# Layer 0's output turned by DMA and VectorE on its way to layer 1, with TensorE's steps put in a new order

## The chip, the cores and the metric

The kernel runs on one core of a Trainium2 chip. The metric is the device time of one execution in microseconds. The kernel before takes 2156.92 us, the median of three runs (2154.6 to 2158.59).

## What is computed

A stack of four graph layers over 128 graphs of 64 nodes with 256 features each, in float32. Each layer adds its result to its input and normalises every row:

```
x = layernorm(x + L0(x))     # attention over all node pairs that the adjacency allows, one head
x = layernorm(x + L1(x))     # attention over a list of 512 edges, four heads
x = layernorm(x + L2(x))     # graph convolution, two dense layers with batch normalisation
x = layernorm(x + L3(x))     # two graph convolutions, then four short LSTMs over windows
```

Only layers 0 and 1 matter here. Layer 0 computes, with `Wh = x W`,

```
e = leaky_relu(s1[i] + s2[j]);  e = -inf where adj is 0
x1 = layernorm(x + softmax(e) Wh)
```

Layer 1 starts with two products of `x1`, the queries `x1 W_lin^T` and the values `x1 W_val^T`. Per edge and head it forms leaky-relu scores, takes a softmax over the edges of one source node, sums the weighted values, and multiplies by `W_out^T`.

## The kernel before

**Tiles.** The 8192 rows (graph and node) are cut into NQ = 16 tiles q of 512 rows, held "token-major" as four blocks of 128 rows by 256 features. One tile is 8 graphs (GQ). A big SBUF tile `A` has a slot of 1024 floats per partition for each q; the slot takes layer 0's output of that q (`token_major`, line 208), later layer 2's input. A matmul contracts over partitions, so both layers first need their tile turned: features on the partitions, rows along the free axis (`xT`).

**How it is turned.** There are two ways in the code. `transposed` (line 198) has TensorE make eight 128x128 transposes (line 204) into two PSUM banks, and ScalarE copy them out (line 205). The other is used for layer 0's input from q=1 on: `load_x` (line 126) loads x twice, once plainly into `xin`, and once with eight DMAs (lines 131 to 135) that place each 32x32 square of x, as it is, where the transposed square belongs, in slot q of `A`; then VectorE turns all squares with one `transpose` (line 220), which works within squares of 32x32. Layer 1's tile is turned by TensorE for every q (`l1_t`, line 283).

**Steps.** For layer 0: `l0_a` turns, `l0_b` multiplies by W (16 matmuls, line 230), `l0_c` makes scores and exponentials (one TensorE transpose, line 241; VectorE lines 244 to 248, 254; ScalarE line 251), `l0_d` transposes the exponentials (line 260), `l0_e` multiplies by Wh (line 270), adds x on VectorE and normalises: statistics on VectorE (lines 92 to 95), a power and the scaling on GpSimd (lines 83, 97), into slot q of `A`; last it asks for x of q+2. For layer 1: `l1_t` turns, `l1_qv` makes queries and values in two halves (lines 295 and 298), `l1_graph` one graph's edge scores (two matmuls, line 332, and a ScalarE pass, line 334), `sums` adds them over heads (line 323). Two tiles q form a superblock S of the softmax: `l1_softmax` (line 342 on TensorE, scans on VectorE, lines 344 to 351, an exponential on ScalarE), `l1_sums` (two more scans, lines 357 and 358), `l1_weights` (two sets of transposes, line 366; VectorE lines 372 and 374; four indirect stores into a DRAM table by GpSimd, line 378; two loads back, line 384). Three or four iterations later `v_a`, `v_b`, `v_c` weight the values, multiply by W_out (line 413), add and normalise (line 415 and the layernorm) and store the result (line 418), and prepare layer 2's input (line 433).

**Order.** The loop over q (lines 659 to 676) goes through eight graphs b. After each `l1_graph` it makes the steps of `between[b]`. `step` (line 643) ties every step's TensorE instructions behind the last one of the step before, so TensorE's order is exactly the one written. On the other engines a scheduler in the compiler sets the order, by the order of tracing and by what it reckons to be ready; each engine then works through its list in order. SyncE issues almost all DMAs, also in order.

**Buffers.** PSUM's eight banks: three named "m", which nearly all steps share in turn, two pairs named "z" and one named "e". `tT`, the turned tile, has one buffer that both layers use; `xin` has two.

Of the kernel before, what the change touches and what calls it, by code (L numbers as in the profile page):

```python
# [8 lines left out]
F32 = mybir.dt.float32  # L9
# [8 lines left out]
P = 128  # L18
NB = 128
N = 64  # L20
D = 256
KD = D // P
# [4 lines left out]
NQ = 16  # L27
PQ = 4
QT = 512
# [12 lines left out]
def kernel(ctx: ExitStack, tc: tile.TileContext, i, out):  # L42
    nc = tc.nc
# [4 lines left out]
    dram = ctx.enter_context(tc.tile_pool(name="dram", bufs=1, space=DRAM))  # L48
# [3 lines left out]
    A = main.tile([P, NQ, 2 * QT], F32, name="A")  # L52
# [59 lines left out]
    with ExitStack() as two:  # L112
        wa = two.enter_context(tc.tile_pool(name="wa", bufs=1))
        values, ph = ExitStack(), ExitStack()
        vp = values.enter_context(tc.tile_pool(name="vp", bufs=1, side="right"))
        psm = values.enter_context(tc.tile_pool(name="psm", bufs=1, space=PSUM, side="right"))
        xp = ph.enter_context(tc.tile_pool(name="xp", bufs=2))
        work = ph.enter_context(tc.tile_pool(name="work", bufs=2))
        ps = ph.enter_context(tc.tile_pool(name="ps", bufs=1, space=PSUM))

        def bank(shape, name="m", bufs=3):
            return (psm if name == "m" else ps).tile([P] + shape, F32, name=name, bufs=bufs)

        xin = {}

        def load_x(q):
            xin[q] = xp.tile([P, PQ, D], F32, name="xin")
            nc.sync.dma_start(xin[q], x_view[q])
            if q:

                rows = i["x"][q * QT:(q + 1) * QT, :].rearrange("(j t) (k i f) -> i k t j f", t=32, k=KD, f=32)
                for n in range(4):
                    for k in range(KD):
                        to = A[n * 32:(n + 1) * 32, q, k * QT:(k + 1) * QT]
                        nc.sync.dma_start(to.rearrange("t (j f) -> t j f", f=32), rows[n, k])

        class su:

# [27 lines left out]
        for s in range(2):  # L166
            nc.sync.dma_start(bd[s * N:(s + 1) * N, s * N:(s + 1) * N], i["adj"])
        load_x(1)

        wq = wa.tile([P, KD, D + HEADS], F32, name="wq")  # L170
        wv = wa.tile([P, KD, D], F32, name="wv")
# [22 lines left out]
        def own(q, shape, name):  # L194

            return work.tile(shape, F32, name=name, bufs=1) if q else su.tile(shape, F32, name)

        def transposed(src, q=1):

            t = own(q, [P, KD, QT], "tT")  # L200
            for k in range(KD):
                p_ = bank([PQ, P])
                for c in range(PQ):
                    nc.tensor.transpose(p_[:, c, :], src[:, c, k * P:(k + 1) * P], ident)
                nc.scalar.activation(t[:, k, :], p_.rearrange("p c t -> p (c t)"), AF.Copy)
            return t

        def token_major(q):

            return A[:, q, :].rearrange("p (c d) -> p c d", c=PQ)  # L210


        L0 = {}

        def l0_a(q):
            L0[q] = {"x": xin.pop(q)}
            if q:

                L0[q]["xT"] = work.tile([P, KD, QT], F32, name="tT", bufs=1)
                nc.vector.transpose(L0[q]["xT"].rearrange("p k t -> p (k t)"), A[:, q, :])  # L220
            else:
                L0[q]["xT"] = transposed(L0[q]["x"], q)

        def l0_b(q):
            xT = L0[q]["xT"]
            wh = L0[q]["wh"] = own(q, [P, PQ, D + 2], "wh")
            for c in range(PQ):
                p_ = bank([D + 2])
                for k in range(KD):
                    nc.tensor.matmul(p_, xT[:, k, c * P:(c + 1) * P], w0[:, k, :],  # L230
                                     start=k == 0, stop=k == KD - 1)
                nc.scalar.activation(wh[:, c, :], p_, AF.Copy)

            sb = L0[q]["sb"] = own(q, [P, PQ, P], "sb")
            nc.scalar.activation(sb, wh[:, :, D + 1:].to_broadcast([P, PQ, P]), AF.Copy)

        def l0_c(q):
            wh, sb = L0[q]["wh"], L0[q]["sb"]
            sc = bank([PQ, P])
            for c in range(PQ):  # L240
                nc.tensor.transpose(sc[:, c, :], sb[:, c, :], ident)
            e = L0[q]["e"] = work.tile([P, PQ, P], F32, name="e0")
            for c in range(PQ):
                nc.vector.scalar_tensor_tensor(e[:, c, :], sc[:, c, :], wh[:, c, D:D + 1], mask,
                                               op0=OP.add, op1=OP.add)
            nc.vector.scalar_tensor_tensor(e, e, SLOPE, e, op0=OP.mult, op1=OP.max)
            mx = small.tile([P, PQ], F32, name="mx")
            nc.vector.tensor_reduce(mx, e, AX.X, OP.max, negate=True)
            sm = small.tile([P, PQ], F32, name="sm")
            for c in range(PQ):  # L250
                nc.scalar.activation(e[:, c, :], e[:, c, :], AF.Exp, bias=mx[:, c:c + 1],
                                     accum_out=sm[:, c:c + 1])
            ri = L0[q]["ri"] = small.tile([P, PQ], F32, name="ri")
            nc.vector.reciprocal(ri, sm)
# [9 lines left out]
        def l0_e(q):  # L264
            x, wh, eT, ri = (L0[q][n] for n in ("x", "wh", "eT", "ri"))
            for c2 in range(2):
                p_ = bank([2, D])
                for c in range(2):
                    g = 2 * c2 + c
                    nc.tensor.matmul(p_[:, c, :], eT[:, g, :], wh[:, g, :D], start=True, stop=True)  # L270
                for c in range(2):
                    g = 2 * c2 + c
                    nc.vector.scalar_tensor_tensor(x[:, g, :], p_[:, c, :], ri[:, g:g + 1], x[:, g, :],
                                                   op0=OP.mult, op1=OP.add)
            layernorm(token_major(q), x, PQ, nc.gpsimd)
            L0.pop(q)
            if q + 2 < NQ:
                load_x(q + 2)


        L1 = {}

        def l1_t(q):
            L1[q] = {"xT": transposed(token_major(q)), "qs": [],
                     "v": vp.tile([P, PQ, D], F32, name="v", bufs=5)}

        def l1_qv(q, c2):
            xT, v = L1[q]["xT"], L1[q]["v"]

            sp = spads[q // BPS % 2].rearrange("p (s e x b d h) -> p s e x b d h", e=2, s=2, x=2, b=BPS, d=2)  # L290
            pv = bank([2, D])
            for c in (2 * c2, 2 * c2 + 1):
                pq = bank([D + HEADS])
                for k in range(KD):
                    nc.tensor.matmul(pq, xT[:, k, c * P:(c + 1) * P], wq[:, k, :],  # L295
                                     start=k == 0, stop=k == KD - 1)
                for k in range(KD):
                    nc.tensor.matmul(pv[:, c % 2, :], xT[:, k, c * P:(c + 1) * P], wv[:, k, :],  # L298
                                     start=k == 0, stop=k == KD - 1)
# [235 lines left out]
        setup_order()  # L535
        l0_c(0)
        l0_a(1)
        setup_ends()
        l0_b(1)
# [98 lines left out]
        LAG = BPS + 1  # L638
# [20 lines left out]
        for q in range(NQ):  # L659
            S = q // BPS - 1 if q % BPS == 0 else -1  # L660
            between = [
                [(l0_e, q + 1), (l0_a, q + 2)],
                [(sums, q if q else -1), (l1_softmax, S)],
                [(l1_sums, S), (l0_b, q + 2)],
                [(v_b, q - LAG - 1)],
                [(l1_weights, S), (l1_t, q + 1), (l0_c, q + 2)],
                [(sums, q), (l1_qv, q + 1, 0)],
                [(v_c, q - LAG - 1), (v_a, q - LAG)],
                [(l0_d, q + 2), (l1_qv, q + 1, 1)],
            ]  # L670
# [64 lines left out]
        q = 0  # L735
# [90 lines left out]
    work = ctx.enter_context(tc.tile_pool(name="work3", bufs=2, reuse_waits="tile"))  # L826
# [290 lines left out]
```

## Time and profile before

| | |
|---|---|
| time, median of 3 runs | 2156.92 us |
| TensorE matmuls busy | 2066.8 us (96%) |
| VectorE busy | 881.6 us (41%) |
| ScalarE busy | 931.1 us (43%) |
| GpSimd busy | 418.7 us (19%) |
| packets under 512 bytes | 150192 of 232637 |
| loop over q | 50.98 us (first graph of q=0) to 517 us (last) |
| TensorE, VectorE busy in 223.17 to 255.92 us (q=6) | 30.29 and 23.15 of 32.75 us |
| one turn on VectorE, 128x1024 (line 220) | 1245 ns |
| one transpose on TensorE, 128x128 (line 204) | 273 ns, median |

The profile is one execution. Busy shares are averages over stages with different limits, so a change in one stage is read from that stage alone, here from the timelines of the engines between 50 and 520 us. In a timeline, each row is a group of like instructions: start, time from the first start to the last end, engine, line and operation, tiles, count, and in brackets how long the engine stood idle before it and what ended the wait. Matmuls overlap in the records, so the cost of a group on TensorE is read from its start to the next group's start.

### The profile page before, as it was taken

Reading aid. Unit: us, or ns where it says so; the run is one execution under the profiler, and the core shown is the slowest. Engines: PE = TensorE matmul, PEld = TensorE weight load, DVE = VectorE, ACT = ScalarE, POOL = GpSimd, SP = SyncE. Lnnn points to the kernel's source line nnn. Section 1 sums busy time; section 2 is a strip of 40 time slices with the busy share of each in tenths; the row PEclk is TensorE's granted clock in tenths of the full one; section 3 lists DMA queues with packets and bytes.
Section 4 is the critical chain, followed back from the end, with each engine's and each line's share of the span. In section 5 each row is a group of like instructions: output and inputs, shape, how many; then the busy total and the mean of one; then the engine's idle time right before and its main releaser. Section 6 shows DMA issues by size and latency. Waiting matters only on the chain.

```text
span 2156.5 us, 29415 instructions
## 1 busy us (share of the span) xinstructions
PE 2066.8 (96%) x11343; PEld 1329.6 (62%) x11343; DVE 881.6 (41%) x2069; ACT 931.1 (43%) x1795; POOL 418.7 (19%) x569
## 2 busy tenths in 40 slices
PE   5999999998999979999999999999999999999998
PEld 4666767665544444685576576577477478468466
DVE  7456665654444344233234233323323423423223
ACT  2776666664349064333334234334333333333332
POOL 1133334333200011021111111111111211202012
PEclk8999999999999979999999999999999999999999
DMA  5244531322240022012012112111201202202001
GB/s 154 51 68 80 85 58 48 53 40 43 44 123 20 0 88 79 1 55 81 22 50 69 40 34 64 59 29 55 74 11 59 88 6 60 72 1 59 20 3 56
DMA packets 232637, 113.42 MB, mean 53 GB/s; under 512 B 150192, under 2 KB 215728, under 8 KB 232240
## 3 DMA queue, kind: packets, MB, share of 16 engines
q1 hardware_dynamic: 230640, 109.57, 20.1%
q8 instruction: 89, 1.46, 0.3%
q0 software_dynamic: 1024, 1.05, 0.2%
q10 hardware_dynamic: 832, 0.92, 0.1%
q14 instruction: 52, 0.43, 0.1%
HBM read 67.45 MB, written 44.04 MB: 52 GB/s over the span
## 4 chain that ended last, share of the span: by engine, by line
PE 81%; DVE 7%; ACT 5%; DMA 3%; issue 2%; POOL 1%; SPq 0%; ACTq 0%; DVEq 0%; POOLq 0%
PE l L982 32%; PE l L988 19%; PE pz L719 5%; PE pz L784 4%; PE e L323 3%; PE g L921 2%; PE g L933 2%; PE m L295 2%; PE z L332 2%; PE m L298 2%; PE m L230 2%; PE g L878 1%; PE m L413 1%; DMA way<-st 1%; ACT A L891 1%
## 5 line engine op out<-in xcount | busy, mean ns | idle before, releaser
L982 PE MATMUL l<-H,wih 128*128 128x256 f32 (+2 forms) x2496 | 789.2, 471 | 11.3 <-DVE H L1011 6.1
L982 PEld LDWEIGHTS l<-H,wih 128*128 128x128 f32 x2496 | 469.9, 190 | 304.2 <-issue 188.7
L988 PE MATMUL l<-hid,whh 128*128 128x256 f32 (+2 forms) x1536 | 436.2, 437 | 1.2 <-DVE hid L1011 1.2
L988 PEld LDWEIGHTS l<-hid,whh 128*128 128x128 f32 x1536 | 291.8, 190 | 130.0 <-issue 61.2
L994 ACT ACTIVATE gate_i<-l,bias 128x256 f32<-128x256 f32 (+2 forms) x176 | 100.0, 568 | 515.1 <-PE l L988 440.3
L997 DVE TENSOR_TENSOR gate_i<-gate_i,gate_g 128x256 f32<-128x256 f32 (+2 forms) x96 | 48.4, 504 | 423.6 <-ACT gate_g L994 423.6
L998 POOL TENSOR_TENSOR cell<-gate_f,cell 128x256 f32<-128x256 f32 (+2 forms) x96 | 84.2, 877 | 666.1 <-ACT gate_f L994 666.1
L83 POOL TENSOR_TENSOR ln_rs<-ln_rs,mhalf 128x2 f32<-128x2 f32 (+2 forms) x97 | 78.0, 804 | 662.8 <-DVE ln_rs L95 662.5
L334 ACT ACTIVATE u<-z 128x1024 f32<-128x1024 f32 x128 | 130.3, 1025 | 64.3 <-PE z L332 63.3
L994 ACT ACTIVATE gate_g<-l,bias 128x256 f32<-128x256 f32 (+2 forms) x176 | 100.2, 569 | 100.3 <-PE l L982 52.0
L1002 ACT ACTIVATE gate_g<-cell 128x256 f32<-128x256 f32 (+2 forms) x176 | 90.0, 511 | 90.4 <-DVE cell L999 44.7
L994 ACT ACTIVATE gate_o<-l,bias 128x256 f32<-128x256 f32 (+2 forms) x176 | 99.2, 564 | 62.0 <-PE l L988 54.1
L719 PE MATMUL pz<-A,w 128*128 128x512 f32 x256 | 113.1, 595 | 0.0
L1001 DVE TENSOR_TENSOR cell<-gate_i,gate_g 128x512 f32<-128x512 f32 (+2 forms) x80 | 50.2, 627 | 142.5 <-ACT gate_g L994 142.3
L332 PE MATMUL z<-gath_r,qs 128*128 128x512 f32 x256 | 100.9, 482 | 0.6 <-ACT u L334 0.4
L306 DVE TENSOR_TENSOR qs<-m,qs 64x256 fp32r<-64x256 f32 x128 | 54.1, 422 | 109.0 <-ACT qs L305 106.9
L719 PEld LDWEIGHTS pz<-A,w 128*128 128x128 f32 x256 | 47.9, 190 | 55.4 <-issue 53.4
L295 PE MATMUL m<-wq,tT 128*128 128x260 f32 x256 | 72.5, 407 | 8.1 <-ACT yT L403 5.4
L994 ACT ACTIVATE gate_f<-l,bias 128x256 f32<-128x256 f32 (+2 forms) x96 | 51.0, 531 | 60.0 <-PE l L988 60.0
L1011 DVE TENSOR_TENSOR hid<-gate_o,gate_g 128x256 f32<-128x256 f32 (+2 forms) x96 | 48.4, 504 | 67.5 <-ACT gate_g L1002 39.5
L1011 DVE TENSOR_TENSOR H<-gate_o,gate_g 128x512 f32<-128x512 f32 (+1 forms) x64 | 40.9, 640 | 80.0 <-PE l L982 67.8
L721 DVE BATCH_NORM_STATS2 st<-pz 128x6 f32<-128x512 f32 x64 | 44.4, 697 | 59.5 <-PE pz L719 59.4
(242 smaller groups left out, 2518.4 us busy)
## 6 DMA issues: line engine op xcount, KB each, us to landing
way<-st SPq DMA_DIRECT2D x59, 256.0 KB
st<-way SPq DMA_DIRECT2D x236, 64.0 KB
xin<-in_x SPq DMA_DIRECT2D x16, 512.0 KB
ld<-table SPq DMA_DIRECT2D x16, 512.0 KB
x_dram<-y SPq DMA_DIRECT2D x16, 512.0 KB
x2r<-x_dram SPq DMA_DIRECT2D x32, 256.0 KB
x_dram<-A SPq DMA_DIRECT2D x64, 128.0 KB
x3r<-x_dram SPq DMA_DIRECT2D x64, 128.0 KB
```

The costliest lines, as they stand in the source:

```text
L83: nc.gpsimd.tensor_tensor(dst, dst, mhalf[:, :n], OP.pow)
L295: nc.tensor.matmul(pq, xT[:, k, c * P:(c + 1) * P], wq[:, k, :], start=k == 0, stop=k == KD - 1)
L332: nc.tensor.matmul(z[:, k, :], L1[q]["qs"][c][:, s, k * P:(k + 1) * P], gath_r, start=True, stop=True)
L334: nc.scalar.activation(u, z, AF.Relu)
L719: nc.tensor.matmul(p_, w1[:, k, m * P:(m + 1) * P], A[:, q, k * QT:(k + 1) * QT], start=k == 0, stop=k == KD - 1)
L784: nc.tensor.matmul(p_, w2[:, k, m * P:(m + 1) * P], hidden(q, k), start=k == 0, stop=k == M1 - 1)
L982: nc.tensor.matmul(gates[n], wih[p][:, k, mw * P:(mw + 1) * P], Hw[:, k, :, s, :], start=k == 0, stop=not s and k == KD - 1)
L988: nc.tensor.matmul(gates[n], whh[p][:, k, m * P:(m + 1) * P], hid[:, k], start=False, stop=k == KD - 1)
L994: nc.scalar.activation(act[n], gates[n], AF.Tanh if n == "g" else AF.Sigmoid, bias=bias[:, p - 1, m:m + 1])
L998: nc.gpsimd.tensor_tensor(cell[:, j], act["f"], cell[:, j], OP.mult)
L1002: nc.scalar.activation(act["g"], cell[:, j], AF.Tanh)
L1011: nc.vector.tensor_mul(Hw[:, jj, :, s, :] if over else new[:, jj], o, t)
```

## The change

Layer 1 gets its turned input as layer 0 does, from q=2 on (TURN = 2; q=0 and 1 keep TensorE's transposes, in both layers). `l0_e(q)` writes its normalised tile to a DRAM tile x1 and loads it back with the eight square-placing DMAs, into slot q+1 of `A` (or, for the last two q, a buffer of `xin`). `l1_t(q)` is then one VectorE transpose, placed behind the last VectorE instruction traced before it. This takes the eight transposes off TensorE and the two copies off ScalarE.

Layer 0's own squares are now loaded one q at a time (`load_xT(q + 1)` at the end of `l0_b(q)`), and turned into slot q+1 of `A` in place of `tT`. `l0_e(q)` thus comes when slot q+1 is free again.

Since x1 now travels through DRAM, layer 0's steps come earlier against layer 1's: `l0_b` at the first graph, `l0_c` at the fourth, `l0_d` at the sixth, `l0_e(q + 2)` at the seventh graph of iteration q rather than at the first of q+1. TensorE's larger steps are spread over the eight graphs.

```diff
         def load_x(q):
             xin[q] = xp.tile([P, PQ, D], F32, name="xin")
             nc.sync.dma_start(xin[q], x_view[q])
-            if q:
-
-                rows = i["x"][q * QT:(q + 1) * QT, :].rearrange("(j t) (k i f) -> i k t j f", t=32, k=KD, f=32)
-                for n in range(4):
-                    for k in range(KD):
-                        to = A[n * 32:(n + 1) * 32, q, k * QT:(k + 1) * QT]
-                        nc.sync.dma_start(to.rearrange("t (j f) -> t j f", f=32), rows[n, k])
+
+        TURN = 2
+
+        def load_squares(to, rows):
+
+            rows = rows.rearrange("(j t) (k i f) -> i k t j f", t=32, k=KD, f=32)
+            for n in range(4):
+                for k in range(KD):
+                    part = to[n * 32:(n + 1) * 32, k * QT:(k + 1) * QT]
+                    nc.sync.dma_start(part.rearrange("t (j f) -> t j f", f=32), rows[n, k])
+
+        def load_xT(q):
+
+            load_squares(A[:, q, :], i["x"][q * QT:(q + 1) * QT, :])
...
         load_x(1)
+        load_xT(2)
...
         def l0_a(q):
             L0[q] = {"x": xin.pop(q)}
-            if q:
-
-                L0[q]["xT"] = work.tile([P, KD, QT], F32, name="tT", bufs=1)
-                nc.vector.transpose(L0[q]["xT"].rearrange("p k t -> p (k t)"), A[:, q, :])
-            else:
+            if q < TURN:
                 L0[q]["xT"] = transposed(L0[q]["x"], q)
+                return
+
+            t = A[:, q + 1, :] if q + 1 < NQ else work.tile([P, KD * QT], F32, name="tT", bufs=1)
+            nc.vector.transpose(t, A[:, q, :])
+            L0[q]["xT"] = t.rearrange("p (k t) -> p k t", k=KD)
...
             nc.scalar.activation(sb, wh[:, :, D + 1:].to_broadcast([P, PQ, P]), AF.Copy)
+            if TURN <= q + 1 < NQ:
+                load_xT(q + 1)
...
             layernorm(token_major(q), x, PQ, nc.gpsimd)
             L0.pop(q)
+            if q >= TURN:
+
+                x1 = dram.tile([QT, D], F32, name="x1_dram", bufs=2)
+                nc.sync.dma_start(x1.rearrange("(c p) d -> p c d", p=P), token_major(q))
+                sq[q] = A[:, q + 1, :] if q + 2 < NQ else xp.tile([P, PQ, D], F32, name="xin").rearrange(
+                    "p c d -> p (c d)")
+                load_squares(sq[q], x1)
             if q + 2 < NQ:
                 load_x(q + 2)
...
         def l1_t(q):
-            L1[q] = {"xT": transposed(token_major(q)), "qs": [],
-                     "v": vp.tile([P, PQ, D], F32, name="v", bufs=5)}
+            L1[q] = {"qs": [], "v": vp.tile([P, PQ, D], F32, name="v", bufs=5)}
+            if q < TURN:
+                xT = transposed(token_major(q))
+                L1[q]["xT"] = [[xT[:, k, c * P:(c + 1) * P] for c in range(PQ)] for k in range(KD)]
+                return
+            xT = work.tile([P, KD, QT], F32, name="tT", bufs=1)
+
+            with tc.issue_after([t for t in nc.cur_bb.bb.instructions if t.engine == mybir.EngineType.DVE][-1]):
+                nc.vector.transpose(xT.rearrange("p k t -> p (k t)"), sq.pop(q))
+            L1[q]["xT"] = [[xT[:, k, c * P:(c + 1) * P] for c in range(PQ)] for k in range(KD)]
...
             between = [
-                [(l0_e, q + 1), (l0_a, q + 2)],
+                [(l0_b, q + 2)],
                 [(sums, q if q else -1), (l1_softmax, S)],
-                [(l1_sums, S), (l0_b, q + 2)],
-                [(v_b, q - LAG - 1)],
-                [(l1_weights, S), (l1_t, q + 1), (l0_c, q + 2)],
-                [(sums, q), (l1_qv, q + 1, 0)],
-                [(v_c, q - LAG - 1), (v_a, q - LAG)],
-                [(l0_d, q + 2), (l1_qv, q + 1, 1)],
+                [(l1_sums, S), (v_b, q - LAG - 1)],
+                [(l0_c, q + 2)],
+                [(l1_weights, S), (l1_t, q + 1), (v_c, q - LAG - 1)],
+                [(sums, q), (l0_d, q + 2), (l1_qv, q + 1, 0)],
+                [(v_a, q - LAG), (l0_a, q + 3 if q + 4 < NQ else -1), (l0_e, q + 2)],
+                [(l1_qv, q + 1, 1), (l0_a, q + 3 if q + 4 == NQ else -1)],
             ]
+            if q == 0:
+                between[0] = [(l0_e, 1), (l0_a, 2), (l0_b, 2)]
```

More of the change, by code (lines that the diff above doesn't have):

```diff
@@ L128, in load_x @@
             nc.sync.dma_start(xin[q], x_view[q])
-            if q:
-                rows = i["x"][q * QT:(q + 1) * QT, :].rearrange("(j t) (k i f) -> i k t j f", t=32, k=KD, f=32)
-                for n in range(4):
-                    for k in range(KD):
-                        to = A[n * 32:(n + 1) * 32, q, k * QT:(k + 1) * QT]
-                        nc.sync.dma_start(to.rearrange("t (j f) -> t j f", f=32), rows[n, k])
+        TURN = 2
[7 more added lines that the diff above has]
+            load_squares(A[:, q, :], i["x"][q * QT:(q + 1) * QT, :])
+        sq = {}
         class su:
@@ L294, in l1_qv @@
                 for k in range(KD):
-                    nc.tensor.matmul(pq, xT[:, k, c * P:(c + 1) * P], wq[:, k, :],
+                    nc.tensor.matmul(pq, xT[k][c], wq[:, k, :],
                                      start=k == 0, stop=k == KD - 1)
                 for k in range(KD):
-                    nc.tensor.matmul(pv[:, c % 2, :], xT[:, k, c * P:(c + 1) * P], wv[:, k, :],
+                    nc.tensor.matmul(pv[:, c % 2, :], xT[k][c], wv[:, k, :],
                                      start=k == 0, stop=k == KD - 1)
```

## The prediction

> **What bounds the kernel now.** I read the page first: span, slices, chain.
>
> ```profile
> span 2156.5 us, 29415 instructions
> ...
> PE   5999999998999979999999999999999999999998
> ...
> DVE  7456665654444344233234233323323423423223
> ...
> PE 81%; DVE 7%; ACT 5%; DMA 3%; issue 2%; POOL 1%; SPq 0%; ACTq 0%; DVEq 0%; POOLq 0%
> ```
>
> TensorE is nearly full and carries 81% of the chain. The change touches only the loop over q (l1_graph and what lies between its graphs), which is the first ten of the 40 slices. So I work by iteration of q. The start of every 16th z matmul (line 332) gives the periods: from q=4 on 32.75 us for each even q and 28.49 us for each odd one (q=6 begins at 223.17, q=7 at 255.92). q=1, 2, 3 and 14 take 24.99, 29.57, 24.68 and 31.46. Even iterations carry the softmax of a superblock as well.
>
> The timeline of TensorE in q=6, second half of the gap between softmax and queries:
>
> ```profile
> 227.97 1.12 PE L342 MATMUL e<-gath,spad 128*128 128x512 f32 x2
> ...
> 237.70 0.60 PE L366 MATMUL m<-ident,dn 128*128 128x128 f32 x4
> 238.97 0.64 PE L204 MATMUL m<-ident,A 128*128 128x128 f32 x4 [0.66 <-issue]
> 240.29 0.66 PE L204 MATMUL m<-ident,A 128*128 128x128 f32 x4 [0.69 <-ACT tT L205]
> 241.43 0.66 PE L241 MATMUL m<-ident,sb 128*128 128x128 f32 x4 [0.48 <-DVE ln_mv L93]
> ...
> 244.34 1.14 PE L295 MATMUL m<-wq,tT 128*128 128x260 f32 x4
> ```
>
> L204 is what goes. TensorE idles 1.8 us around it here, because VectorE holds the PSUM banks: the softmax's scans, v_b's normalisation and the weights queue on it. L295, the queries, begins 21.17 us into the iteration.
>
> q=14 already runs without l0_b between softmax and weights, as every even q will after the change:
>
> ```profile
> 472.96 1.12 PE L342 MATMUL e<-gath,spad 128*128 128x512 f32 x2
> ...
> 481.95 1.06 PE L366 MATMUL m<-ident,dn 128*128 128x128 f32 x4 [2.25 <-DVE dn L358]
> ...
> 486.45 3.07 PE L323 MATMUL e<-u,apad 128*32 128x512 f32 x16
> ```
>
> TensorE waits 2.25 us for VectorE's scan, and L323 then takes 3.07 us instead of 1.92. The windows say why (sixth column: granted clock):
>
> ```profile
> 479.00:482.00 3.00, 0.71 (x5) 0.51 (x6) 2.98 (x4) 0.99 (x1) 0.28 (x1) 1.00 0.00 0
> 482.00:488.80 6.80, 6.11 (x26) 3.31 (x30) 4.26 (x15) 2.22 (x3) 2.83 (x4) 0.50 0.02 5
> ```
>
> VectorE is full where TensorE waits (2.98 of 3.00 us), and the clock is halved for 6.8 us afterwards. The 2.07 us wait at 119.5 to 121.6 (q=2) was followed by 3.4 us at 0.50.
>
> **What the Trainium skill says.** "VectorE: DVE Perf Modes", section "The three transpose paths": VectorE turns only blocks of 32x32 and writes to SBUF, TensorE turns 128x128 into PSUM. So the DMA must put the squares in place, and no copy out of PSUM is left; the trace agrees, L220 turns 128x1024 in 1.245 us. "TensorE: Matmul & The Clock Gate", section "What's actually happening": an idle window of some 3.4 us halves the clock; the trace shows that 2.1 to 2.3 us of idling is enough. "DMA: Bandwidth & Descriptors", section "Two DMAs through the same engine are not ordered": the issuing engine must wait for the write's semaphore before it reads back, so SyncE will stand still for x1. No run here shows that pair.
>
> **Part by part.**
>
> *Removed:* for l1_t(2) to l1_t(15), 8 transposes, 0.87 us of TensorE (207.91 to 208.78), and two copies on ScalarE (hidden, it is busy 21 of 33 us). With the idling beside them (even q 1.83, and 0.53 to 0.56 in each q before the second queries) the most to be won is 14x0.87 + 7x2.39 + 7x0.53 = 33 us.
>
> *Added on VectorE:* one turn of 1.25 us per q, behind all VectorE instructions traced before it: l0_c's reciprocal in odd q, the last at (line 374) in even q. Behind it wait the queries (L295), and TensorE's order is fixed, so everything.
>
> *Even q, from its first z.* Steps up to L342: z 0.65, l0_b 3.30, z 0.75, sums 1.86 = 6.56. From L342 to the end of the last at, VectorE needs 13.30 us in q=14 (472.96 to 486.26), full throughout:
>
> ```profile
> 474.12 0.69 DVE L344 TENSOR_TENSOR e<-e,lb 128x512 f32<-128x512 f32 x1 [0.45 <-PE e L342]
> ...
> 485.60 0.66 DVE L374 SCALAR_TENSOR_TENSOR at<-m,count,rd 128x64 f32<-128x64 f32 x3
> ```
>
> l0_c now comes ahead of the weights and pushes 2.57 us into that queue (242.33 to 244.90: L244, L246, L248). With the turn: 6.56 + 13.30 + 2.57 + 1.25 = 23.7, against 21.17 before. Moving l0_e and l0_a to the iteration before doesn't help: VectorE then idles ahead of L342, and the queue starts there. What follows the queries' start: first queries 3.40, z 0.74, v_a 1.18, l0_e 1.54, z 0.57, second queries 3.55 = 11.0 (v_c moves ahead of them). Even period 34.7, that is +1.9. TensorE has only 17.7 us of work before the queries (6.56, L342 0.56, four more z 2.8, v_b 3.26, L241 0.36, L366 0.87, v_c 0.98, sums 1.85, L260 0.43), so it idles 6 us in pieces of about 2; by what q=14 shows I add one half-clock stretch of 3.4 us on working TensorE, +1.7 (none to two: 0 to 3.4). Per even q +3.6, bounds 1.9 to 5.3.
>
> *Odd q.* v_b begins at 0.65 + 3.30 + 0.75 + 1.85 + 0.65 = 7.2. In q=5 its start is followed 9.99 us later by the end of l0_c's reciprocal (203.99 to 213.98). Plus the turn: 18.45, and 11.0: 29.45, that is +1.0. TensorE's work before it is 16.0, so it idles 2.4 us, on the edge of a halved clock: 0 to 1.7, I take 0.3.
>
> *Added DMA.* Per q a 512 KB write, and 8 DMAs of 512 packets of 128 bytes.
>
> ```profile
> 257.30 3.37 SPq L384 DMA_DIRECT2D ld<-table  x2
> ...
> 275.06 4.68 SPq L135 DMA_DIRECT2D A<-in_x  x8
> ```
>
> Eight squares take 4.3 to 4.7 us to issue, and the last packets move 2.6 us after the last issue (221.37 to 224.0): 6.5 us. xin, 512 KB in rows of 1 KB like x1, took 3.8 us from issue to last packet. x1 itself: l0_e's VectorE work ends 5.2 us after L270 starts, GpSimd's normalisation takes 3.3 to 5.6. In an odd q, x1 is ready about 3 to 5 us after the start; but SyncE first issues the table's loads of the even q before it, whose 8224 packets fill the engines for 7.4 us (share 1.36 in the windows, 258.2 to 265.6). They are released by the fourth indirect store, 12 to 14 us after at: about at the odd q's start. So x1 lands at 11 to 12, the squares at 17 to 18.5, the turn ends at 18.3 to 19.8: 0 to 1.4 us later than VectorE's queue alone, I take 0.7. Odd q: +2.0, bounds 1.0 to 4.1. Even q have 8 us of slack for it.
>
> *q=1 to 3* have no v_b and so a shorter way to the queries, while the squares take as long. q=1: 5.2 + 3.3 + 3.8 + 6.5 + 1.25 = 20 us after L270 begins, against 17.5 of TensorE's work from there to the queries; with the transposes gone that is +0.2, with clock +1. q=2: VectorE's queue, +2.5. q=3, with the first table loads ahead of x1: queries at 17 to 20 instead of 14, +4.5. Sum +8. *q=14* has no l0 work: 3.25 + 13.30 + 1.25 = 17.8, then 9.5, and 1.7 of clock as now: 29 to 31, -1.5. *Setup:* l0_a(1) goes back to TensorE, 8 transposes for a 1.25 us turn; squares of q=2 are loaded instead of q=1. Nothing: VectorE, busy 41 of the first 54 us, is what counts there.
>
> Sum: five even q (4 to 12) 18, five odd (5 to 13) 10, +8, -1.5 = 34.5; 2156.9 + 34.5 = 2191, which I state as 2190.
>
> **Rivals.** *A, faster:* TensorE stays the bound, the queue on VectorE is shorter than I add it up (l0_c fits into gaps or is sequenced behind the weights), the squares are in time. Then two thirds of the 33 us come: 2135. For it: TensorE carries the chain, and VectorE is only 23 of 33 us busy in q=6. Against it: the 2.25 us at L366 in q=14, with less on VectorE than there will be. *B, the squares bound:* SyncE is in order; if x2's store (waits for GpSimd) or the squares of x get ahead of x1's, each of 14 iterations waits some 3 us more, with half clock: 2190 + 40 = 2230. For it: in q=6 four of the squares stood behind x2's store for 6.6 us (239.84 to 246.45). Against it: x1 is ready before x2. *C, even:* gains in TensorE's work and odd q pay for the even ones: 2157, within 4.
>
> **Chances.** Main case 0.50, A 0.27, B 0.16, C 0.07. Main and B are slower (0.66), C the same, A faster. The main case alone spans 2171 (no halved clock, squares in time) to 2215. Range 2138 to 2216: it reaches into A's smaller gains (about 0.1 left below) and leaves B out above (0.1).
>
> **What would show it.** Right: the transposes of `transposed` down from 136 matmuls to 32, even periods of 34 to 37 us, L366 waiting about 2 us for scan dn, L295 waiting for VectorE's turn, granted clock below 1.00 all through 130 to 480 us, where it is 1.00 now. DMA-bound (B): the turn waits for squares in even q too. Wrong: even periods below 32 us with TensorE closed up and clock 1.00; then the step that adds l0_c and the turn to the weights' queue fails.

## The result and the profile after

The changed kernel takes 2243.03 us, the median of four runs (2241.24 to 2243.73), against 2157.68 for the kernel before, the median of four runs beside it. The ratio is 1.0397 (95% interval 1.0379 to 1.0415). It is slower, as forecast, but by 85 us where 33 were forecast, and the time lies above the stated range of 2138 to 2216.

The page of the kernel after, the lines that answer to those shown of before:

```profile
span 2239.2 us, 29455 instructions
...
PE   6878888888799997999999999999999999999998
...
DVE  7445545555344434423423423423423423423223
...
PE 81%; DVE 6%; ACT 6%; DMA 2%; POOL 2%; issue 2%; SPq 1%; POOLq 0%; DVEq 0%; ACTq 0%
```

In the first ten slices TensorE has fallen from nine tenths to eight, though eight transposes per q are gone, and VectorE is no fuller. No engine has become the bound by its work; TensorE waits more. By the first z matmul of each q (line 360 here), even q last 40.1 us instead of 32.75 (mean of 4 to 12: 40.14) and odd q 35.05 instead of 28.49. The loop starts at 45.08 us instead of 50.98, 5.9 us earlier.

The sum agrees with the traces: five even q at +7.4 are 37.0, five odd ones at +6.55 are 32.8, q=0 to 3 add 17.6, q=14 adds 2.8, the start takes off 5.9; together +84.3. So q=15 starts at 583.78 instead of 499.62; what follows it is 1.5 us shorter, and the two spans differ by 82.7.

TensorE's timeline in q=8, an even q that begins at 324.29 (start, time, engine, line, operation, tiles, count, in brackets the wait and what ended it):

```profile
327.60 2.88 PE L241 MATMUL m<-w,A 128*128 128x258 f32 x12 [1.13 <-ACT spad L335]
...
332.72 1.12 PE L370 MATMUL e<-gath,spad 128*128 128x512 f32 x2
...
341.60 0.63 PE L394 MATMUL m<-ident,dn 128*128 128x128 f32 x4 [2.04 <-DVE dn L386]
345.41 1.24 PE L461 MATMUL z<-aht,y 64*64 64x64 f32 x32 [3.18 <-POOL y L97]
...
349.24 3.11 PE L351 MATMUL e<-u,apad 128*32 128x512 f32 x16
...
352.77 1.04 PE L323 MATMUL m<-wq,tT 128*128 128x260 f32 x4
```

L394 is the weights' transposes: its wait for the scan is the one forecast, at 2.04 us. The longest wait is a different one. L461 is v_c, and it waits 3.18 us for the rows that GpSimd normalises after v_b (L441). Behind it L351, the sums over heads, takes 3.11 us instead of 1.92. The queries (L323) begin 28.5 us into the iteration; the forecast was 23.7.

VectorE's timeline in the same stretch shows that the queries did not wait for the turn; behind it VectorE itself had nothing to do for 2.99 us:

```profile
347.71 1.23 DVE L312 STREAM_TRANSPOSE tT<-A 128x1024 f32<-128x1024 f32 x1
351.93 0.18 DVE L267 RECIPROCAL ri<-sm 128x4 f32<-128x4 f32 x1 [2.99 <-ACT e L264]
```

The turn (L312) ended at 348.94, 24.65 us into the iteration, close to the forecast 23.7, and no DMA held it. It was 3.8 us too early to matter.

The chain of waits over this stretch, in order of time (start, us, what), tells why v_c was late:

```profile
340.32 1.13 DVE dn L386
341.45 0.64 DVE ln_st L92 x2
...
343.71 0.98 POOL ln_rs L83
...
344.79 2.07 POOL y L97 x3
```

v_b starts at 334.15. Its statistics (L92) stand on VectorE behind the softmax's scan (L386); then GpSimd makes a power (L83) and scales block by block (L97), and the second half of v_c's matmuls follows at 346.91. VectorE's queue thus bounds v_c as well, by a longer way than it bounds the weights.

The windows of the kernel after (stretch, its length, busy time and count of PE, PEld, DVE, ACT and POOL, then the granted clock, the DMA share and GB/s): behind that wait, then at and behind the wait of the next odd q:

```profile
344.80:351.60 6.80, 5.93 (x78) 3.17 (x82) 4.14 (x8) 3.28 (x9) 3.68 (x5) 0.50 0.22 83
377.60:382.40 4.80, 1.96 (x53) 1.24 (x51) 3.55 (x13) 2.94 (x8) 2.99 (x5) 1.00 0.80 126
382.40:385.80 3.40, 3.38 (x40) 1.47 (x34) 1.42 (x2) 2.58 (x6) 0.21 (x1) 0.50 0.43 160
```

Behind these waits come 6.8 and 3.4 us at half clock (0.50). The Trainium skill, "TensorE: Matmul & The Clock Gate", section "What's actually happening", halves the clock after an idle window of some 3.4 us; here it is halved when TensorE has been busy 1.96 of 4.80 us, after one wait of 2.69. The measurement decides: gaps shorter than the page's window are enough.

The odd q=9 begins at 364.37. TensorE's timeline:

```profile
373.37 3.62 PE L441 MATMUL m<-wout,yT 128*128 128x256 f32 x16
...
381.04 2.33 PE L461 MATMUL z<-aht,y 64*64 64x64 f32 x64 [2.69 <-POOL y L97]
...
387.44 1.04 PE L323 MATMUL m<-wq,tT 128*128 128x260 f32 x4
```

And VectorE's, the turn alone:

```profile
383.34 1.25 DVE L312 STREAM_TRANSPOSE tT<-A 128x1024 f32<-128x1024 f32 x1 [0.20 <-DMA A<-in_x]
```

Again v_c waits, and again the turn is over before the queries begin, by 2.85 us. The 0.20 us ahead of the turn are not a price of the squares: q=5 and q=11 have the same 0.20 with no DMA named, and the squares of q=9 were issued by 377.56, 5.8 us before the turn.

### The profile page after: what moved, and what is told of

It reads as the page before. It is cut to its first block, busy times and chain, and to the rows that moved or that the text cites. A ratio compares the mean times of both kernels' runs of the same rounds, so it can differ in the third digit from the quotient of the medians.

```text
span 2239.2 us, 29455 instructions
## 1 busy us (share of the span) xinstructions
PE 2090.0 (93%) x11239; PEld 1333.4 (60%) x11239; DVE 891.4 (40%) x2082; ACT 923.3 (41%) x1769; POOL 405.8 (18%) x569
## 4 chain that ended last, share of the span: by engine, by line
PE 81%; DVE 6%; ACT 6%; DMA 2%; POOL 2%; issue 2%; SPq 1%; POOLq 0%; DVEq 0%; ACTq 0%
PE l L1012 31%; PE l L1018 18%; PE pz L749 5%; PE pz L814 4%; PE e L351 3%; PE g L951 2%; PE g L963 2%; PE m L323 2%; PE m L241 2%; PE z L360 2%; PE m L326 2%; PE g L908 1%; DMA way<-st 1%; PE m L441 1%; PE m L283 1%
## 5 line engine op out<-in xcount | busy, mean ns | idle before, releaser
L83 POOL TENSOR_TENSOR ln_rs<-ln_rs,mhalf 128x2 f32<-128x2 f32 (+2 forms) x97 | 78.3, 808 | 709.9 <-DVE ln_rs L95 709.7
L360 PE MATMUL z<-gath_r,qs 128*128 128x512 f32 x256 | 105.6, 501 | 1.7 <-DVE qs L334 1.0
L351 PE MATMUL e<-u,apad 128*32 128x512 f32 x512 | 74.8, 710 | 1.5 <-ACT u L362 1.5
L323 PE MATMUL m<-wq,tT 128*128 128x260 f32 x256 | 69.9, 397 | 6.4 <-DVE tT L312 4.7
L241 PE MATMUL m<-w,A 128*128 128x258 f32 x224 | 57.2, 400 | 19.6 <-ACT spad L335 13.9
```

What stands on the lines that cost most here:

```text
L323: nc.tensor.matmul(pq, xT[k][c], wq[:, k, :], start=k == 0, stop=k == KD - 1)
L351: nc.tensor.matmul(pes[S][n * CG:(n + 1) * CG, :], apad[:, k, CG - HEADS - r0:2 * CG - HEADS - r0], u[:, k, :], start=r0 == 0 and k == 0, ...
L360: nc.tensor.matmul(z[:, k, :], L1[q]["qs"][c][:, s, k * P:(k + 1) * P], gath_r, start=True, stop=True)
```

## The experiments

All kernels but one only move steps or change how a tile is turned, and all compute the whole result. Each ratio is to the kernel before, run beside it; its median was 2157.7 to 2160.4 us from round to round, so a difference of 3 us between kernels of different rounds says nothing. The changed kernel wasn't run beside the experiments; differences to it are to its 2243.03 us. In the texts of what was expected, e1 is experiment 1, and so on.

**1. v_c back to its old graph.** Only this step of the changed kernel is moved.

```diff
-                [(l1_weights, S), (l1_t, q + 1), (v_c, q - LAG - 1)],
+                [(l1_weights, S), (l1_t, q + 1)],
...
-                [(v_a, q - LAG), (l0_a, ...), (l0_e, q + 2)],
+                [(v_c, q - LAG - 1), (v_a, q - LAG), (l0_a, ...), (l0_e, q + 2)],
```

> The changed kernel with one step put back: v_c stands at the seventh graph again, ahead of v_a, as before the change. Theory 1 (v_c, brought close behind v_b, waits for GpSimd's normalised y, 2.7 to 3.2 us in every q, and the wait halves the clock): the wait at v_c is gone; an odd q gets 1.8 us and an even q 2.3 us shorter, because the next wait in line (the exponentials of l0_c, then VectorE's turn) ends only 3 us earlier, and half as much again comes back from the clock: 2200 to 2215 us. Theory 2 (the queue on VectorE behind the softmax is the bound and would hold TensorE to the same moment anyway): 2235 to 2245 us.

Measured: 2213.72 us, ratio 1.0253 (1.0235 to 1.0271), 29 us less than the changed kernel and inside the range of the first theory. Its waits for GpSimd are gone, but the next ones stand close behind. TensorE's timeline in q=8, then in q=9:

```profile
330.95 0.72 PE L394 MATMUL m<-ident,dn 128*128 128x128 f32 x4 [2.03 <-DVE dn L386]
...
337.14 1.63 PE L273 MATMUL m<-ident,e 128*128 128x128 f32 x4 [1.64 <-ACT e L264]
...
371.23 1.15 PE L323 MATMUL m<-wq,tT 128*128 128x260 f32 x4 [1.32 <-DVE tT L312]
```

The wait for the scan still halves the clock (L351 at 3.04), then l0_d waits for the exponentials, which follow l0_c on VectorE; in odd q the queries now do wait for the turn. So v_c's place costs at least 29 us, and undoing it inside this order brings the queue on VectorE to light.

**2. The new order with TensorE's transposes.** `l1_t` turns on TensorE for all q, x1 is not written; the table of steps stays.

```diff
-            if q >= TURN:
+            if False:
                 x1 = dram.tile([QT, D], F32, name="x1_dram", bufs=2)
...
-            if q < TURN:
+            if True:
                 xT = transposed(token_major(q))
```

> The changed kernel's order of steps, but layer 1's tile turned by TensorE as before, no x1 in DRAM and no turn on VectorE. Theory 1 and 2 (the new order costs the time, not the way through DRAM): TensorE gets 14 x 0.9 us more to do, part of it in time in which it waits for y: 2240 to 2258 us. Theory 3 (the way through DRAM, its DMAs and the turn on VectorE cost it): most of the 85 us comes back, 2160 to 2190 us.

Measured: 2224.6 us, ratio 1.0300 (1.0282 to 1.0317); it lies between the two ranges and in neither. So the order, with layer 0's new loading, costs 65 us without any turn of layer 1 on VectorE, and the way through DRAM with that turn another 18 in this order, although it takes work off TensorE. Of the 18, 6.8 are q=3, where the squares of x1 were late. The turn's row in q=3 of the changed kernel, on VectorE's timeline; the queries behind it waited 3.36 us (the row names in_x, but the squares of x1, issued from 152.26 to 156.30, are what the turn reads; those of x come after them):

```profile
158.59 1.25 DVE L312 STREAM_TRANSPOSE tT<-A 128x1024 f32<-128x1024 f32 x1 [2.24 <-DMA A<-in_x]
```

The odd q are 1.9 us shorter here. l0_b waits 0.29 us instead of 1.35 for its PSUM banks, and v_b begins 7.7 instead of 9.0 us into q=9; that is 1.3 of them. From v_b to v_c it is 7.67 us in both kernels: here TensorE's transposes stand in the wait for GpSimd, so taking them off wins nothing. In the even q they do push v_c back, to 12.9 us after v_b instead of 11.3, which uses up what l0_b gains. `l1_t` on TensorE takes two of the shared banks in turn and so shifts which bank l0_b gets; that this is why l0_b waits less was not tried by itself.

**3. Dummy work ahead of v_c.** The only kernel with added work: eight matmuls whose result is not used, written into the banks that v_c takes next, so that TensorE doesn't idle while it waits.

```diff
+                for _ in range(8):
+                    nc.tensor.matmul(both[:, 0, :], gath_r[:, :P], gath_r, start=True, stop=True)
```

> The changed kernel with eight more 128x512 matmuls (gath_r on itself, about 2.7 us) ahead of v_c, into the bank pair that v_c then overwrites: TensorE works instead of idling while it waits for y. If the halved clock after each wait costs what its records say (8.5 of 75 us of two iterations at half clock, so some 4 us), the time falls although work was added: 2200 to 2225 us. If the clock costs nothing beyond the wait: 2243 to 2250 us.

Measured: 2232.82 us, ratio 1.0337 (1.0318 to 1.0356): 10 us less than the changed kernel, with 96 matmuls more. The direction was expected, the size was less; the time lies between the two ranges. TensorE's timeline in the same odd q, where v_c is L463 and the dummies (377.64, 2.11 us) end just ahead of it:

```profile
380.11 2.07 PE L463 MATMUL z<-aht,y 64*64 64x64 f32 x64 [0.36 <-POOL y L97]
...
382.77 1.92 PE L351 MATMUL e<-u,apad 128*32 128x512 f32 x16
```

The window behind it, columns as above:

```profile
382.20:385.60 3.40, 3.40 (x25) 1.54 (x26) 1.26 (x2) 2.22 (x3) 0.00 (x0) 1.00 0.39 154
```

v_c starts as late as without the dummies; what differs is the clock: 1.00 instead of 0.50, z and L351 in 2.52 us instead of 3.65, v_c in 2.0 instead of 2.3. An odd q lasts 33.64 us instead of 35.05. Even q stay at 40.2. There 3.4 us at half clock are left, instead of 6.8 or more: in q=4 and q=10 behind the wait for the scan, ahead of the dummies, in q=6, 8 and 12 behind two short waits at v_c. So the halved clock costs 1.4 us of an odd q's 6.6; the rest is waiting, at v_c and at l0_b, and what it pushes back.

**4. v_c early in the kernel before.** The reverse of the first: the kernel before with this one step moved from the seventh graph to the fifth.

```diff
-                [(l1_weights, S), (l1_t, q + 1), (l0_c, q + 2)],
+                [(l1_weights, S), (l1_t, q + 1), (l0_c, q + 2), (v_c, q - LAG - 1)],
                 [(sums, q), (l1_qv, q + 1, 0)],
-                [(v_c, q - LAG - 1), (v_a, q - LAG)],
+                [(v_a, q - LAG)],
```

> The kernel before with one step of the change alone: v_c at the end of the fifth graph's steps (behind l0_c) instead of at the seventh. Theory 1: y is ready 9.4 us after v_b's first matmul, v_c would start after about 5.5 to 6.5, so it waits 3 to 4 us in each of 12 iterations, and the clock halves after it; 2195 to 2220 us. Theory 2 (v_c's place is of no weight): 2155 to 2165 us.

Measured: 2218.08 us, ratio 1.0267 (1.0248 to 1.0286), as expected. One step, moved two graphs forward in a kernel that is otherwise the one before, costs 59 us: even q go from 32.75 to 38.1, odd ones from 28.49 to 33.7. TensorE in an odd q:

```profile
290.48 2.07 PE L433 MATMUL z<-aht,y 64*64 64x64 f32 x64 [2.46 <-POOL y L97]
...
293.50 3.17 PE L323 MATMUL e<-u,apad 128*32 128x512 f32 x16
```

The 5.2 us of an odd q are in and between these rows: 2.46 of waiting; 1.0 because v_c lasts 1.99 us to the next row, fed by GpSimd block by block, where it takes 0.98 with its operand ready; 0.4 and 1.25 because the z matmuls and L323 run at half clock (1.03 and 3.1 us to the next row instead of 0.66 and 1.86).

**5. l0_b behind the softmax.** The first experiment's kernel, with l0_b moved from the first graph to behind the softmax's first matmuls in the second, so that the softmax starts earlier on VectorE and l0_b's banks are free.

```diff
-                [(l0_b, q + 2)],
-                [(sums, q if q else -1), (l1_softmax, S)],
+                [],
+                [(sums, q if q else -1), (l1_softmax, S), (l0_b, q + 2 if q else -1)],
```

> The run e1 (v_c at the seventh graph) with l0_b moved from the first graph to just behind l1_softmax at the second. Theory 2 (in even q the next bound is VectorE's queue behind the softmax: scans, l0_c, weights, turn): the softmax starts 3.3 us earlier, l0_b fills the wait for the scan, an even q gets 3 to 5 us shorter; an odd q 0 to 1 us (l0_b no longer right behind the second queries): 2180 to 2195 us. If the queue is not the bound: 2205 to 2214 us.

Measured: 2187.75 us, ratio 1.0131 (1.0114 to 1.0148), as expected, 26 us less than the first experiment. In q=8 L394 waits 0.16 us instead of 2.03, and L351 is back at 1.92; what is left is l0_d's wait for the exponentials:

```profile
314.34 0.66 PE L394 MATMUL m<-ident,dn 128*128 128x128 f32 x4 [0.16 <-DVE y L443]
...
319.98 1.48 PE L273 MATMUL m<-ident,e 128*128 128x128 f32 x4 [2.66 <-ACT e L264]
```

Two steps moved, v_c and l0_b, have thus taken back 55 of the 85 us, with the way through DRAM left as it is.

**6 and 7. An order with slack, with both ways of turning.** Order: layer 0's `l0_a(q + 2)` and `l0_e(q + 1)` at the first graph again, `l0_b` after `l1_sums`, the second queries at the fourth graph of the next iteration, `l0_c` behind the weights, v_c at the seventh graph, turn and first queries last. Experiment 6 keeps x1's way through DRAM and VectorE's turn, experiment 7 has TensorE's transposes.

```diff
+                [(l0_a, -1 if last else q + 2), (l0_e, q + 1)],
+                [(sums, q if q else -1), (l1_softmax, S)],
+                [(l1_sums, S), (l0_b, -1 if last else q + 2)],
+                [(v_b, q - LAG - 1), (l1_qv, q if q else -1, 1)] + [...] * last,
+                [(l1_weights, S), (l0_c, q + 2)],
+                [(sums, q)],
+                [(v_a, q - LAG), (v_c, q - LAG - 1)],
+                [(l0_d, q + 2), (l1_t, q + 1), (l1_qv, q + 1, 0)],
```

> The way through DRAM and the turn on VectorE kept, in another order of steps, near that of before: l0_a and l0_e at the first graph, l0_b at the third, v_b and the second half of q's own queries at the fourth, weights and l0_c at the fifth, v_a and v_c at the seventh, l0_d, the turn and the first half of the queries of q+1 at the eighth. So v_c has 5 us more after v_b, the weights 6 us more after the softmax, the turn the whole iteration after l0_e. If the places of the steps cost the time and the way through DRAM does not: TensorE loses its transposes and some of its waits, 2115 to 2150 us. If the way through DRAM costs it: 2160 to 2200 us, with VectorE's turn waiting for its squares.

> The order of e6, with layer 1's tile turned by TensorE and no x1 in DRAM. The difference to e6 is the price of the turn alone. If VectorE's turn is worth what TensorE's transposes take (14 x 0.87 us) and a little waiting: 12 to 25 us above e6. If the DMAs and the turn cost as much as they save: within 5 us of e6.

Measured: 2174.13 us (1.0072; 1.0053 to 1.0091) and 2185.9 (1.0122; 1.0105 to 1.0140). VectorE's turn is worth 11.8 us here, just under the first range of experiment 7's forecast. But experiment 7 is itself 26 us above the kernel before, with the same way of turning, so this order costs more than the turn wins.

Divided by 14 q the 11.8 us look like the 0.87 us of transposes and nothing else, but that is an average over unlike stages. From q=4 to 13 even q last 32.8 us in experiment 6 against 36.2 in 7, odd ones 30.6 against 31.8: 23 us in ten q, more than the transposes take. q=2 and q=15 (up to its last z) alone give back 3.2 and 3.7, and another 3.9 lie behind the loop, where the two kernels don't differ. In q=9 of experiment 7 the queries begin 3.28 us after the first transpose, 2.14 of them a wait for ScalarE's copies, and 3.4 us at half clock follow, as in each q from 8 to 13; in experiment 6 they begin after a wait of 1.41 for the turn, and the clock stays at 1.00. So here the turn did take away idling beside the transposes too. The waits of TensorE between 150 and 520 us (in total, times, longest), in experiment 6, with VectorE's turn:

```profile
PE m L323 <- DVE tT L312: 15.4, 11, 1.4
```

and in experiment 7, with TensorE's:

```profile
PE m L323 <- ACT tT L215: 22.6, 11, 2.1
```

Experiment 6 itself fell into the upper of its two ranges, but not for the reason given there: the turn did not wait for its squares, it stood behind layer 0's reciprocal, which waits 1.72 us for ScalarE's exponentials. VectorE's timeline in q=8 of experiment 6:

```profile
317.67 0.18 DVE L267 RECIPROCAL ri<-sm 128x4 f32<-128x4 f32 x1 [1.72 <-ACT e L264]
318.04 1.25 DVE L312 STREAM_TRANSPOSE tT<-A 128x1024 f32<-128x1024 f32 x1 [0.20 <-issue]
```

So an engine's own queue, not the DMA, held the turn. What VectorE's turn would be worth in the unchanged order of the kernel before was not tried.

**8 to 11. Taking the remaining waits away one at a time.** Experiment 8 makes the reciprocal only in l0_e, behind layer 1's turn. Experiment 9 also moves `l0_a` to the end of the iteration before and puts the reciprocal behind that turn too. Experiment 10 is 8 with the reciprocal behind layer 0's turn too, experiment 11 is 10 with `l0_d` behind the first queries.

```diff
-            ri = L0[q]["ri"] = small.tile([P, PQ], F32, name="ri")
-            nc.vector.reciprocal(ri, sm)
+            L0[q]["sm"] = sm
...
+            ri = small.tile([P, PQ], F32, name="ri")
+            with tc.issue_after(turned[0]) if turned else ExitStack():
+                nc.vector.reciprocal(ri, sm)
```

> The run e6, with l0_c's reciprocal (which waits for ScalarE's exponentials) moved to l0_e and put behind layer 1's turn on VectorE. In e6 TensorE waits 1.4 us in 12 of the iterations for the turn, which stands behind that reciprocal. If the place in VectorE's queue is the reason: the wait goes, 12 to 18 us less than e6, 2156 to 2163 us. If the turn would wait for its squares anyway: 2170 to 2176 us.

Experiment 9 against 8, the order alone:

```diff
-                [(l0_a, -1 if last else q + 2), (l0_e, q + 1)],
+                [(l0_a, -1 if q else 2), (l0_e, q + 1)],
...
-                [(l0_d, q + 2), (l1_t, q + 1), (l1_qv, q + 1, 0)],
+                [(l0_d, q + 2), (l1_t, q + 1), (l1_qv, q + 1, 0), (l0_a, q + 3 if q + 4 < NQ else -1)],
```

> The run e8, with l0_a (layer 0's own turn) at the end of the iteration before and ahead of l0_e on VectorE. In e6 l0_b waits 1.5 us for it in every odd q from 5 on. If that is the queue again: 6 to 10 us less than e8, 2147 to 2156 us, and so below the kernel before. If the squares of x come too late for that: as e8 or slower.

Experiments 10 and 11 against 8; the second change is in 11 alone:

```diff
-            with tc.issue_after(turned[0]) if turned else ExitStack():
+            if turned:
+                last_turn = [i for i in nc.cur_bb.bb.instructions if i.engine == mybir.EngineType.DVE][-1]
+            with tc.issue_after(last_turn) if turned else ExitStack():
                 nc.vector.reciprocal(ri, sm)
...
-                [(l0_d, q + 2), (l1_t, q + 1), (l1_qv, q + 1, 0)],
+                [(l1_t, q + 1), (l1_qv, q + 1, 0), (l0_d, q + 2)],
```

> The kernel of e8 (layer 1's turn ahead of layer 0's reciprocal, 2168.97 us), with the reciprocal now tied behind layer 0's turn of the same graph as well, so that the turn that feeds l0_b stands first on VectorE. In e8 the first matmul of l0_b waited 1.70 us for that turn in odd q, in seven or so iterations. Theory 1 (the wait is only an order on VectorE): it goes, and layer 0's additions end 1.2 us later, which nobody waits for: 1.3 us less in each of the six odd q from 3 on: 2158 to 2163. Theory 2 (TensorE's fixed order has the next bound right behind each one): l0_e's PSUM banks come free 1.2 us later and the wait moves to another matmul on the m banks: 2166 to 2172.

> e10 with l0_d behind the first query and value block instead of ahead of it. In e8 that block waited 0.78 us for ScalarE's copy of the exponentials' transposes in 10 iterations between 150 and 520 us. Theory 1: that wait goes and l0_e, one graph later, has its operand in time: 0.78 us in 13 iterations, 10 us less than e10: 2148 to 2154, faster than the kernel before. Theory 2: ScalarE's copy now stands behind the copies of the queries and values, l0_e waits for it some 0.6 us or more, and nothing is won: 2158 to 2165.

Measured: 2168.97 us (1.0048; 1.0026 to 1.0069), 2179.45 (1.0091; 1.0074 to 1.0108), 2175.76 (1.0080; 1.0052 to 1.0109) and 2186.3 (1.0124; 1.0107 to 1.0141). Only 8 seems to gain on 6, 5 us where 12 to 18 were expected, and the two intervals overlap; its time lies between its two ranges. 9 is slower than 8, as its second forecast has it, but not because squares came late: l0_b waits for its turn there in one q only, the last with layer 0's steps. 10 and 11 lie above both of their ranges. Whether 10 differs from 8 is not settled by the times; in the traces its odd q are 1.0 us shorter (29.6 against 30.58) and most of its even ones 1.5 longer. 9 and 10 differ only in l0_a's place, and TensorE's waits in them are nearly the same: what l0_a's earlier place brings beside the reciprocal's is too small to see. Each time the wait aimed at went and another appeared. The waits of TensorE between 150 and 520 us, in experiment 8:

```profile
PE m L326 <- ACT eT L274: 7.8, 10, 0.8
```

and in experiment 11, where l0_d had moved to be rid of this wait:

```profile
PE m L287 <- ACT eT L274: 15.1, 11, 1.4
```

Now l0_e waits for the same copy, and l0_d (L272) waits 13.9 us for ScalarE's copy of the queries: 29 us in place of 8. In these orders, fixed by hand, moving the step that waited only showed the next wait. No order tried with the turn on VectorE beats the kernel before.

## Why the prediction was right in its direction and wrong in its size

The two iterations in the forecast's own terms, in us:

| even q | forecast | measured (q=8) |
|---|---|---|
| to the softmax's first matmul, L370 | 6.56 | 8.43 |
| from there to the end of VectorE's turn | 17.12 | 16.22 |
| end of the turn to the queries | 0 | 3.83 |
| queries to the next z | 11.0 | 11.60 |
| half clock, added apart | 1.7 | in the rows above |
| sum | 36.4 | 40.1 |

| odd q | forecast | measured (q=9) |
|---|---|---|
| to v_b | 7.2 | 9.00 |
| v_b to the end of the turn | 11.25 | 11.22 |
| end of the turn to the queries | 0 | 2.85 |
| queries to the next z | 11.0 | 11.98 |
| squares and half clock, added apart | 1.0 | in the rows above |
| sum | 30.45 | 35.05 |

**The step that failed** is the one that takes the end of VectorE's turn for the start of the queries (23.7 and 18.45 us), and in it "v_c moves ahead of them", with v_c as 0.98 us of TensorE's work. In the kernel before v_c comes 11.8 us after v_b in an odd q and waits for nothing. TensorE's timeline of before, q=7:

```profile
265.23 3.61 PE L413 MATMUL m<-wout,yT 128*128 128x256 f32 x16
...
277.02 1.16 PE L433 MATMUL z<-aht,y 64*64 64x64 f32 x64
```

GpSimd scales the first of its rows there from 271.99 on, 6.8 us after v_b and 5 us ahead of v_c, so nothing had to wait for it. In the new order TensorE is ready for v_c about 5 us after v_b in an odd q (373.37 to 378.36, where the z matmuls before it end) and 8.1 in an even one (334.15 to 342.23), while GpSimd has the first rows ready only 7.7 and 11.3 us after v_b. The forecast priced the steps that moved by their work and asked only of VectorE what they wait for; it names what stands behind the turn, but not what v_c stands behind. Experiment 4 shows that this one move costs 59 us without any other part of the change, experiment 1 that at least 29 of the 85 are due to it in the new order. The 59 and the 29 differ because in the new order other waits, those of VectorE's queue, come right behind and take over when v_c's is gone. So the even periods, 34 to 37 us by the signs of being right, came out at 40.1.

**Mis-sized: l0_b.** It was costed as 3.30 us directly behind the second queries. It takes 4.80 (325.33 to 330.13), and 0.22 more before it, since it waits 1.35 us for ScalarE to empty the banks that the queries fill. That is most of the 1.8 to 1.9 us by which L370 and v_b come later than forecast. In the kernel before, other work stood between the two.

**Right: VectorE's queue.** L394 waited 2.04 us for the scan, against "about 2". The queue from L370 to the end of the turn was 16.22 us against 17.12, and in odd q 11.22 against 11.25. Experiment 5 supports that this queue was the next bound in even q: starting it earlier, with l0_b moved out of its way, gave 26 us. But L323 waiting for the turn, named as a sign of being right, was not there in the steady state, because v_c came later still.

**Right in kind, too small in size: the half clock.** From q=2 to 13 the granted clock falls to 0.50 in every q: from q=4 on for 3.4 us in odd q and for 6.8 in even ones (10.2 in q=4 and 6), where one stretch of 3.4 had been taken. For odd q it had been put at 0 to 1.7 us and 0.3 taken; experiment 3 measured 1.4.

**Right: the squares in even q; too dear in odd ones.** SyncE issued x1's squares in q=8 from 332.32 to 336.37, eleven microseconds before the turn. In the odd q=9 they cost nothing that the trace shows, instead of 0.7. The wait for x1's write, which the prediction expected of SyncE, was short: SyncE issued the write at 328.90 in q=8, then loads of x until 331.18, and the first square at 332.32, so it stood still for 1.1 us at most. Rival B, with waits for squares in each of 14 iterations, is wrong in the steady state, though its time of 2230 is the nearest of all; a cause is not confirmed by the sum it would give. Only q=3 had the squares late, and there 8.2 us were lost where 4.5 were forecast, 6.8 of them beside experiment 2, which has no such squares.

**Wrong, too low: q=0 to 2 and q=14.** They add 3.4, 2.4, 3.5 and 2.8 us instead of 0, 1, 2.5 and -1.5. What q=0 to 2 lost was not taken apart. q=14 lasts 27.74 us in experiment 1, 34.28 with v_c in its new place, so v_c's place takes the gain there too.

**Wrong, too high: the setup.** It was costed at nothing, and the loop starts 5.9 us earlier. Experiment 2, without the turn, starts 4.5 us earlier than before (46.45), and experiment 4, which keeps the old way of loading, does not (52.42). So it goes with the new loading, where tile 1 is turned by TensorE and the squares of tile 2 are loaded in place of those of tile 1. Which of the two it is was not separated.

**Rival A** had TensorE as the bound and two thirds of 33 us to be won. Experiments 6 and 7 show that the turn can win TensorE's work and some idling, 11.8 us in all, but against a kernel with the same order and not against the kernel before. How much of the 33 us would come in the order of before stays open.

## What to carry over

When steps move in a fixed order, list for each what its operand passes through (here VectorE's statistics, then GpSimd's power and scaling) and compare that time with the distance to the step that starts it, before counting any engine's work. v_c, one microsecond of work, cost five in each q when it was reached early (experiment 4): everything behind it on TensorE waited and then ran at half clock. And a removed wait is worth only the distance to the next one: v_c's place cost 59 us in the one order, and its undoing gave 29 in the other.

## What the runs showed that was not expected

- Work added to TensorE shortened the kernel: eight unused matmuls in each of 12 iterations, 2.1 us of work each time, put where it would idle, took off 10 us (experiment 3).
- A VectorE operation was more than three times as long beside GpSimd. In experiment 6 the operation of line 259, 0.69 us in most q, took 2.51 to 2.53 us in q=5, 7, 9 and 11, where GpSimd's copy of `am` (L419, 1.99 us) had begun just before it, at 343.26 us in q=9. VectorE's row:

```profile
343.28 2.51 DVE L259 SCALAR_TENSOR_TENSOR e<-e 128x512 f32<-128x512 f32 x1
```

The Trainium skill, "SBUF — State Buffer", section "SBUF: two separate sides", says that a VectorE operation with two SBUF inputs and a GpSimd operation that reads SBUF exclude each other for a whole instruction; the trace agrees, since the 1.82 us added here are about the copy's 1.99. So moving a step can lengthen it by what it now lies beside.
